# Windowed attention at the end of a convolution network: the four quarters' score products given in turn, and the weighted sums in one run

## The chip, the cores and the metric

One core of a Trainium2 chip runs the whole program, and the time is that of one execution in microseconds (us) on the device. The engines of the core have queues of their own and meet only at semaphores: PE is the matmul array, with its weight loads shown apart as PEld; DVE is the vector engine, ACT the scalar engine, POOL the general engine, and SP issues the transfers. Matmuls write PSUM, which here is used as four buffers of two banks each (`bank2`), handed out in turn; a fifth request waits until the first of the four has been read out.

## The reference, cut to what matters

Four layers run over x of shape (8, 56, 56, 192), all in fp32: two gated Toeplitz layers, a ConvNeXt block, and the windowed attention that is changed here. Each layer has a group norm ahead of it and is added to x. The attention, after a roll of the image by 3 rows and columns:

```python
q = x @ Wq; k = x @ Wk; v = x @ Wv
shp = (b, N_HEAD, nw, WS * WS, DIM_V)          # plain reshapes: (8, 6, 64, 49, 32)
q = q.reshape(shp); k = k.reshape(shp); v = v.reshape(shp)
scores = jnp.einsum('bhnqd,bhnkd->bhnqk', q, k) * DIM_V ** 0.5
scores = scores + bias                         # and masks on some windows
attn = jax.nn.softmax(scores, axis=-1)
out = jnp.einsum('bhnqk,bhnkd->bhnqd', attn, v)
out = out.reshape(b, n_h, n_w, -1) @ Wfc + bfc
```

So there are 8 x 384 small problems, each with 49 queries, 49 keys and 32 channels.

## The kernel before, in words

The attention stage (`attention`, from line 1006) is the last of the program. Its work is cut into 16 units: for each of the 8 images two halves `hh`. A unit's channels-by-token arrays `qf` and `kf` have four quarters of the image on the four groups of 32 partitions, and each quarter holds 48 problems. A unit is worked off in three thirds (`g` = 0, 1, 2), each with 16 problems of every quarter.

The four quarters of a third are split in two calls, `i` = 0 and 1. Call `i` of `scores` (line 1198) takes the quarters `i` and `i + 2`: for 8 values of `n`, two halves and two quarters `c`, a product of 32 rows (channels) by 64 columns (queries) with 49 moving columns (keys), 32 products in all, into one `bank2`. Quarter `c` has its own bank, and `half` says which 64 output partitions are written. Still inside `scores` follow the softmax's first part: DVE scales and adds the bias (line 1219) and takes the maxima (1228), POOL subtracts them (1229), ACT takes the exponentials (1230). `divide` follows: DVE sums (1237) and takes reciprocals (1238), POOL multiplies (1239). The probabilities `e` live in a ring of four buffers.

One third later they are used. `turned` transposes one `e` on PE (line 1245) and copies the result out of PSUM, the first call's on DVE (1255) and the second's on ACT (1253). `weighted` (line 1267) makes the sums: per call 32 products of 49 rows by 32 columns with 49 moving columns, into `po`; bank `par` belongs to the row half `par`. `sixths` copies `po` out on DVE (1277) and ACT (1282).

Between these, the loop places pieces of other work by hand through `give`: steps of `project`, the q, k and v products of the next unit (lines 1124, 1134 for v with its copy on ACT at 1142; 1177 for q and k, with copies on DVE at 1192 and ACT at 1190), and the two halves of `out`, the last product of the unit before (line 1293, added to x on DVE at 1304). The table `order` gives for each third how many steps stand at each of four places. In third 0 these are four v steps, in third 2 four q or k steps, in third 1 two q or k steps and both halves of `out`.

Written in order, a third on PE is: scores of call 0, piece 0, scores of call 1, piece 1, both transposes of the late third, piece 2, sums of call 0, piece 3, sums of call 1. PE takes its queue in that order. The framework's scheduler sets the order on DVE, ACT and POOL: on DVE the maxima and the sums of call 0 stand ahead of the scaling (or, in third 0, the maxima) of call 1; the copy of the transposed `e` stands ahead of the sums of call 1 in third 0 and behind them in thirds 1 and 2.

Each fp32 product of the program leaves two pairs of records, each pair a weight load and a matmul. Below, a "pair" is such a pair, so a call of `scores` has 64 pairs.

## Time and profile before

| what | value |
| --- | --- |
| median of 3 runs | 6182.19 us (6163.62 to 6187.67) |
| the profiled execution's own time | 6174.82 us |
| its span, first to last instruction | 6172.7 us |
| mean granted PE clock | 0.964 |
| attention's main loop, in the span | about 5274 to 6140 us |
| PE, PEld, DVE, ACT, POOL busy in 5274 to 6140 (866 us) | 774, 590, 520, 305, 290 us |
| scores, 6144 pairs (L1207) | PE busy 118.0 us |
| weighted sums, 6144 pairs (L1267) | PE busy 91.7 us |
| transposes (L1245) | PE busy 97.8 us |
| q and k steps (L1177) | eight groups of 40 to 59 us |
| v steps (L1124, L1134) | 95.9 and 57.2 us |
| last product (L1293) | 71.6 and 59.3 us |

Matmuls overlap in the array, so a busy figure is less than the count times the mean duration. The thirds of one unit can be told apart in the rows in order of time: third 0 has the rows of lines 1124 and 1134 between its scores, third 1 those of line 1293, third 2 four groups of line 1177.

### The profile page before, as it was taken

The page shows a single profiled execution, that of the slowest core. Times are in us where ns is not written, and L with a number is a line of the kernel's source. Part 1 is how long each engine was busy: PE and PEld are TensorE (multiplying, and loading weights), DVE is VectorE, ACT ScalarE, POOL GpSimd, SP SyncE. Part 2 cuts the span into 40 slices and gives each one's busy share as a digit, 9 for nine tenths or more (in the row PEclk, how much of TensorE's full clock was granted, in tenths as well). Part 3 has the DMA queues.
Part 4 walks back from the last instruction along what each step waited for, and adds up shares of the span by engine and source line. Part 5 has one row for each costly group of instructions (what it writes and reads, how often), then busy time and mean ns, then how long its engine had stood idle before and what let it go on. Part 6 is the DMA issues. An engine that isn't in the chain of part 4 may idle for free.

```text
span 6172.7 us, 151914 instructions
## 1 busy us (share of the span) xinstructions
PE 5666.5 (92%) x68832; PEld 4464.1 (72%) x68832; DVE 2847.8 (46%) x4858; ACT 2153.0 (35%) x2736; POOL 639.2 (10%) x833
## 2 busy tenths in 40 slices
PE   4997999899999999999889989999999999988997
PEld 3776878788778788888778878885665444666666
DVE  6663555444556444456444443242221322556555
ACT  1343444223444333344333332224323333333332
POOL 0000000000000000000000010000000100333332
PEclk9998999999999999999999999999999999999998
DMA  7799998887676788776899956663444322344442
GB/s 251 173 207 251 259 249 229 221 241 236 183 206 185 193 239 241 193 212 180 220 247 247 264 171 224 213 221 128 155 163 139 96 63 61 71 87 96 90 90 59
DMA packets 1139557, 1119.75 MB, mean 181 GB/s; under 512 B 342528, under 2 KB 1076736, under 8 KB 1123488
## 3 DMA queue, kind: packets, MB, share of 16 engines
q1 hardware_dynamic: 1103328, 909.05, 54.6%
q0 software_dynamic: 35584, 200.98, 10.4%
q8 instruction: 541, 8.86, 0.6%
q14 instruction: 104, 0.85, 0.0%
HBM read 753.79 MB, written 389.15 MB: 185 GB/s over the span
## 4 chain that ended last, share of the span: by engine, by line
PE 69%; DVE 9%; DMA 4%; ACT 3%; issue 3%; SPq 2%; POOL 1%; POOLq 0%; DVEq 0%; ACTq 0%
PE bank L256 11%; PE bank L350 7%; PE bank L903 6%; PE bank L467 6%; PE bank L477 5%; PE bank L367 5%; PE bank L764 5%; PE bank L983 4%; PE bank L482 3%; PE bank L499 3%; PE bank L997 3%; DMA qv<-t 2%; PE bank L1124 1%; PE bank L1177 1%; POOL e L1229 1%
## 5 line engine op out<-in xcount | busy, mean ns | idle before, releaser
L256 PE MATMUL bank<-wq,t 64*128 64x256 f32 (+5 forms) x8000 | 1319.6, 372 | 62.9 <-ACT t L239 42.8
L256 PEld LDWEIGHTS bank<-wq,t 64*128 64x128 f32 (+3 forms) x8000 | 1040.1, 189 | 313.4 <-issue 115.6
L275 ACT ACTIVATE t<-t 128x2048 f32<-128x2048 f32 (+1 forms) x300 | 444.2, 1488 | 777.9 <-DVE t L265 764.8
L265 DVE TENSOR_TENSOR t<-bank,wq 128x1024 f32<-128x1024 f32 (+2 forms) x500 | 540.2, 1112 | 254.1 <-PE bank L256 253.3
L357 ACT COPY ot<-bank 128x896 f32<-128x896 f32 x576 | 484.3, 920 | 384.6 <-PE bank L350 380.2
L350 PE MATMUL bank<-q,tm 56*64 56x112 f32 x18432 | 521.2, 265 | 64.2 <-issue 44.0
L511 ACT ACTIVATE t<-bank,wo 128x448 f32<-128x448 f32 x448 | 247.9, 635 | 895.3 <-PE bank L482 870.9
L350 PEld LDWEIGHTS bank<-q,tm 56*64 56x64 f32 x18432 | 479.9, 137 | 100.2 <-issue 70.3
L367 PE MATMUL bank<-ident,ot 120*128 120x120 f32 x4032 | 472.9, 276 | 76.8 <-ACT ot L357 37.2
L278 DVE TENSOR_TENSOR t<-t 128x1024 f32<-128x1024 f32 (+1 forms) x300 | 285.1, 955 | 530.8 <-ACT t L275 451.3
L367 PEld LDWEIGHTS bank<-ident,ot 120*128 120x128 f32 x4032 | 431.8, 145 | 125.9 <-ACT ot L357 42.8
L467 PE MATMUL bank<-t,wo 128*128 128x224 f32 x1792 | 393.2, 375 | 45.3 <-DVE t L449 42.3
L903 PE MATMUL bank<-z,w 128*128 128x448 f32 (+1 forms) x1344 | 413.1, 555 | 1.6 <-ACT h L912 1.6
L521 DVE SCALAR_TENSOR_TENSOR t<-bank,wo,t 128x448 f32<-128x448 f32 x112 | 76.4, 682 | 705.6 <-PE bank L506 705.6
L467 PEld LDWEIGHTS bank<-t,wo 128*128 128x128 f32 x1792 | 349.8, 202 | 63.8 <-issue 39.9
L477 PE MATMUL bank<-t,wo 128*128 128x224 f32 x1792 | 363.2, 356 | 11.3 <-issue 6.8
L538 DVE TENSOR_TENSOR t<-t,t 128x896 f32<-128x896 f32 x224 | 235.8, 1083 | 296.2 <-ACT t L511 296.1
L477 PEld LDWEIGHTS bank<-t,wo 128*128 128x128 f32 x1792 | 340.3, 192 | 19.7 <-issue 13.2
L764 PEld LDWEIGHTS bank<-xt,cm 113*112 113x112 f32 x3072 | 309.2, 178 | 36.9 <-issue 30.8
L903 PEld LDWEIGHTS bank<-z,w 128*128 128x128 f32 (+1 forms) x1344 | 182.2, 189 | 205.0 <-issue 196.8
L383 POOL DMA_DIRECT2D L_sum<-s x288 | 141.1, 496 | 1769.1 <-DVE s L373 1766.3
L764 PE MATMUL bank<-xt,cm 113*112 113x108 f32 (+2 forms) x3072 | 317.4, 263 | 4.3 <-ACT h L912 3.2
(142 smaller groups left out, 6940.1 us busy)
## 6 DMA issues: line engine op xcount, KB each, us to landing
q<-qv SPq DMA_DIRECT2D x36, 3584.0 KB
q<-qv SPq DMA_DIRECT2D x72, 1568.0 KB
L_sum<-s POOLq DMA_DIRECT2D x288, 392.0 KB, 7.6
t<-L_sum SPq DMA_DIRECT2D x112, 1008.0 KB
qv<-t SPq DMA_DIRECT2D x192, 512.0 KB
cm<-in_L_cm SPq DMA_DIRECT2D x96, 896.0 KB
tm<-L_mat SPq DMA_DIRECT2D x72, 896.0 KB
x<-t POOLq DMA_DIRECT2D x112, 336.0 KB, 5.5
```

Source lines behind the costliest of these rows:

```text
L256: nc.tensor.matmul(pp[:m, b, 256 * j : 256 * j + k], x[rows, j, 2 if part else b, s : s + m], w[rows, part, c0 + c : c0 + c + k],  start=p ...
L265: nc.vector.tensor_add(z[:m, c : c + k, :], view(pp[:m], 0, [[1, k], [256, 4]]), view(bias[:m], c0 + c, [[1, k], [0, 4]]),)
L275: nc.scalar.activation(z[:m, :n, :], z[:m, :n, :], AF.Silu)
L278: nc.vector.tensor_mul(prod[:m, :k], half[:, :, 0], half[:, :, 1])
L350: nc.tensor.matmul(pt[64 * s : 64 * s + 64, r, j * 112 : (j + 1) * 112], tm[rows, c * H : c * H + 64], q[rows, PR * s : PR * s + PR, 4 * c ...
L357: nc.scalar.copy(view(ot, 4 * g, [[112 * 32, 2], [32, 112], [1, 4]]), view(pt, 0, [[512, 2], [1, 112], [112, 4]]),)
L367: nc.tensor.transpose(pz[:, i, :120], ot[:120, at : at + 128], self.ident[:120, :120])
L467: mm(gs[c // 2][:, b, c % 2 * 256 : c % 2 * 256 + N], pw[:, 0, 128 * c : 128 * c + 128], xn[:, b], start=c % 2 == 0, stop=False,)
L477: mm(P[:, b, :N], ow[:, c, 0:128], g[:, 4 * b + c], start=c == 0, stop=False)
L511: nc.scalar.activation(pg[:, c], view(gs[i], c * 256, [[512, 2], [1, N]]), AF.Silu, bias=pb[:, 2 * i + c : 2 * i + c + 1],)
L764: nc.tensor.matmul(pc[:, 128 * e + 4 * m0 : 128 * e + 4 * m1], cm[:113, e, k, :], xt[:, m0 - 1 + k : m1 - 1 + k, c + e, :], start=n == 0 a ...
L903: nc.tensor.matmul(phs[c][:, s, :TT], w0[rows, part, at : at + 128], z[rows, Z[2 if part else s], :], start=part == flip, stop=part != flip,)
```

## The change

`scores` is called once for a third and takes two `bank2` at the start. Its innermost loop goes over the four quarters, in the order of partitions 0 to 31, 32 to 63, 64 to 95 and 96 to 127, and then over the two halves, so that eight products in a row go to eight different parts of the array (four row groups by two column halves), each row group with a bank of its own. What followed in `scores` is now `softmax`, called for both halves of the result after all 64 products. Both `divide` calls come after piece 1. `weighted` takes both transposed tiles and alternates between them, so that eight products in a row go to two row halves by four column groups; it runs once, ahead of piece 3, with `sixths` right behind it. The number of products, the pieces and their places are the same. In the changed file line 1207 is still the product of the scores, the scaling is line 1222, the transposes 1248, the weighted sums 1271, the last product 1297.

```diff
@@ -1195,22 +1195,25 @@
                     fs.append(f)
                 return v, fs[0], fs[1]
 
-            def scores(hh, g, i, qf, kf):
-
-
-                s = bank2()
+            def scores(hh, g, qf, kf):
+
+
+                ss = [bank2(), bank2()]
                 for n in range(8):
                     for half in range(2):
-                        for c in range(2):
+                        for i, c in ((0, 0), (1, 0), (0, 1), (1, 1)):
                             qd = slice(32 * (i + 2 * c), 32 * (i + 2 * c) + 32)
                             u = (16 * g + 8 * half + n) * WR
                             nc.tensor.matmul(
-                                s[64 * half : 64 * half + 64, c, n * WR : (n + 1) * WR],
+                                ss[i][64 * half : 64 * half + 64, c, n * WR : (n + 1) * WR],
                                 qf[qd, u : u + 64],
                                 kf[qd, u : u + WR],
                                 start=True,
                                 stop=True,
                             )
+                return [softmax(hh, g, i, s) for i, s in enumerate(ss)]
+
+            def softmax(hh, g, i, s):
                 var = {0: 1, 3: 2}.get((2 * i + 3 * hh + g) % 4, 0)
                 e = ering[count[0] % NE]
                 count[0] += 1
@@ -1255,22 +1258,23 @@
                     nc.vector.tensor_copy(et, ev)
                 return et
 
-            def weighted(g, i, et, v, po):
+            def weighted(g, ets, v, po):
 
                 for m in range(4):
                     for half in range(2):
                         for c in range(2):
-                            for par in range(2):
-                                at = slice(64 * par, 64 * par + WR)
-                                qr = i + 2 * c
-                                u = 4 * half + m
-                                nc.tensor.matmul(
-                                    po[32 * qr : 32 * qr + 32, par, u * WR : (u + 1) * WR],
-                                    v[at, qr, 8 * g + u, :],
-                                    et[at, 4 * c + m, 64 * half : 64 * half + WR],
-                                    start=True,
-                                    stop=True,
-                                )
+                            for i in range(2):
+                                for par in range(2):
+                                    at = slice(64 * par, 64 * par + WR)
+                                    qr = i + 2 * c
+                                    u = 4 * half + m
+                                    nc.tensor.matmul(
+                                        po[32 * qr : 32 * qr + 32, par, u * WR : (u + 1) * WR],
+                                        v[at, qr, 8 * g + u, :],
+                                        ets[i][at, 4 * c + m, 64 * half : 64 * half + WR],
+                                        start=True,
+                                        stop=True,
+                                    )
 
             def sixths(g, po, ot, oj):
 
@@ -1363,14 +1367,12 @@
                                 got = step(gen)
                         return got
 
-                    es = []
+                    es = scores(hh, g, qf, kf) if n < len(units) else []
                     for i in range(2):
-                        if n < len(units):
-                            es.append(scores(hh, g, i, qf, kf))
                         now = give(i)
                         self.norm_part()
-                        if n < len(units):
-                            divide(es[i])
+                    for e in es:
+                        divide(e)
                     if late is not None:
                         g_late, es_late, v_late = late
                         ets = [turned(e, i) for i, e in enumerate(es_late)]
@@ -1380,11 +1382,9 @@
                             ot = self.at2.tile([128, HR], F32, name="ot", bufs=1)
                             oj = self.at2.tile([128, 6, HT], F32, name="oj", bufs=1)
                         po = bank2()
-                        weighted(g_late, 0, ets[0], v_late, po)
+                        weighted(g_late, ets, v_late, po)
+                        sixths(g_late, po, ot, oj)
                     now = give(3)
-                    if late is not None:
-                        weighted(g_late, 1, ets[1], v_late, po)
-                        sixths(g_late, po, ot, oj)
                     late = (g, es, v) if es else None
                     if g == 0 and n + 3 == len(units) // 2:
                         for more in self.all_norms():
```

## The prediction

> **What bounds it now.** I read the page first, then the busy time of each engine in the attention's main loop, then PE's rows in order of time, then the chain of waits over one unit. The page says that PE is the busy engine of the whole program:

> ```profile
> PE 5666.5 (92%) x68832; PEld 4464.1 (72%) x68832; DVE 2847.8 (46%) x4858; ACT 2153.0 (35%) x2736; POOL 639.2 (10%) x833
> ```

> The change touches only the last 866 us, so that stage must be read by itself. The table of stretches (span, then busy us of PE, PEld, DVE, ACT, POOL, then granted clock, DMA share, GB/s) gives the whole loop, and two stretches that follow each other:

> ```profile
> 5274.00:6140.00 866.00, 774.08 (x21688) 590.12 (x21688) 519.82 (x837) 304.94 (x372) 290.30 (x207) 0.96 0.40 85
> ...
> 5427.90:5431.30 3.40, 1.57 (x49) 0.86 (x40) 1.34 (x2) 2.00 (x3) 1.12 (x1) 1.00 0.03 7
> 5431.30:5438.10 6.80, 6.02 (x146) 4.24 (x149) 2.56 (x5) 0.47 (x1) 1.52 (x1) 0.50 0.01 2
> ```

> PE is busy 89% of the loop; no other engine passes 60%. In the second row PE stands for over half of 3.4 us, and in the third its clock is 0.50: a pause is paid for twice. PE's rows in order of time show what a call costs (start, length of the group, pairs at the end):

> ```profile
> 5358.78 1.57 PE L1267 MATMUL bank<-et,v 49*32 49x49 f32 x128
> 5360.29 0.80 PE L1207 MATMUL bank<-f,f 32*64 32x49 f32 x40
> 5362.48 0.56 PE L1207 MATMUL bank<-f,f 32*64 32x49 f32 x24 [1.40 <-issue]
> ...
> 5470.06 2.50 PE L1293 MATMUL bank<-oj,wfc 32*64 32x224 f32 x88 [0.32 <-ACT f L1190]
> ```

> Two things are to be seen. The sums take 11 ns a pair ((1.57 - 0.2) / 127), an undisturbed call of scores (1.15 us for 64) 15 ns. And a run of such short pairs stops: after 128 + 40 pairs PE waits 1.40 us for nothing but "issue". Beside the pauses lie the packets of the instruction queue, 16 KB each, that is 128 pairs; 171 of them land in the loop. In 24 places a pause of over 1 us ends some 1.4 us after such a packet landed; these are 36 us, and with the shorter ones 47 pauses and 50 us. Instructions arrive too late. In the pause shown the last 128 pairs began at about 5359.25 (40 pairs into the sums), and PE went on at 5362.48: 3.2 us is the least time from the start of one such block to the start of the next.

> The chain of waits shows the rest, from a third 0 into a third 1:

> ```profile
> 5438.85 1.14 PE bank L1207 x64
> ...
> 5453.61 1.12 PE bank L1207 x64
> 5454.83 0.99 DVE e L1219
> 5455.84 0.98 DVE mx L1228
> ...
> 5456.98 1.53 POOL e L1229
> 5458.53 0.88 ACT e L1230
> 5459.43 0.98 DVE sm L1237
> ...
> 5460.61 0.93 DVE e L1219
> 5461.56 0.98 DVE mx L1228
> ...
> 5462.69 1.55 POOL e L1229
> 5464.27 0.88 ACT e L1230
> 5465.18 0.98 DVE sm L1237
> ```

> Third 0 (up to 5453.6) is all PE. Then the chain leaves PE and runs through the softmax of call 0 and, after it, that of call 1, because DVE's queue has the scaling of call 1 (5460.61) behind the sums of call 0. In third 1 this holds up the additions of line 1304 and so the second half of the last product; in third 2 it holds up the copy of the transposed tile, and so the sums.

> **The change, part by part, for one unit.** Times below count from the start of a third's scores.

> Scores. The starts of a call's 64 pairs spread over 0.93 us in the trace; on 4 parts of the array these are 16 rounds of 58 ns, and 0.2 us follow to the next group. With 128 pairs on 8 parts the rounds stay 16: 1.15 us in place of 2.30. That eight products can run is shown by line 1293: 88 pairs of 224 columns, the same 32 by 64 shape over four row groups and two halves, in 2.50 us are (2.50 - 0.35) / 87 = 25 ns a pair, while one pair streams some 190 ns. The bounds are 1.15 us (full gain) and 2.1 us (15 ns a pair as now); I take the first, on the nearest shape.

> Sums. 64 pairs take 0.83 us with the step to the next group; xb's steps of line 1177, in the same 64 by 32 shape over two row halves and four column groups, issue their pairs about 6.7 ns apart. 128 pairs at 6.7 ns and 0.2 us are 1.05 us in place of 1.66. Bounds: 0.9 and 1.55.

> [...]

> Softmax. DVE now has both scalings, both maxima, then (in the thirds with q or k steps) a copy of line 1192, then the sums. With durations and gaps of the chain above: scalings start at 1.3 and 2.3, maxima at 3.3 and 4.3, POOL subtracts 4.45 to 5.97 and to 7.5, ACT's exponentials end at 6.9 and 8.4, the sums at 7.9 and 9.4, the reciprocals at 9.9. The first call's values come later than now, the second's earlier, and POOL and ACT work under DVE. The values are used a third later, so the end of `divide` is covered by some 10 us of work on PE. Two PSUM buffers are now taken at once. In third 0 the one for the sums is that of the second v step, whose copy (0.80 us) on ACT moves behind the second exponential, to 9.2; the sums need it at 11.0 at the earliest. The store of that copy on SP's queue follows as late; it is read a unit later.

> Third 0. Now 5438.85 to 5453.54, 14.7 us. After: PE needs scores 1.15, three pieces and transposes 3 x 2.36 + 1.76, so it is at the sums at 10.0; but the transposed copy (1.09 us) now stands behind the second call's sums on DVE and ends at 11.0. PE waits 1.0, and the piece and the next scores queue behind that wait. Then sums 1.05 and a piece 2.36: 14.45. Nearly nothing gained; the wait replaces the time saved.

> Third 2. Now, without a stop: scaling 1.29, call 0's round 5.78 (5454.83 to 5460.61), call 1's 5.54 (to 5466.15), copy 1.0, so the sums start at 13.6; then 0.83 + 2.36 + 0.83 = 17.6. After: as third 0, 14.45.

> Third 1. Now 5453.54 to 5473.99, 20.45. After: sums and the reciprocal end at 9.7, the additions (2.55) at 12.3, the copies of lines 1192 and 1190 at 13.35, the second half of the last product 2.5, the weighted sums 1.05: 16.9.

> A unit falls from 52.75 to 45.8 us, by 6.95; for 15 full units (the first has no late sums) 104 us. No transfer is added. POOL's and SP's queues keep their work; POOL's two multiplications move behind both subtractions.

> Stops for instructions. The same pairs now come in denser runs: 128 of sums, a piece, 128 of scores. Take third 2 into third 0, with 64 pairs left of the block begun and one block landed: the block ends 0.45 us into the sums and the one after next may start at 3.7; sums and q step use the landed block by 3.4 (0.3 lost), the scores use the next at once (to 4.9), and the following piece waits until 6.95: 2.0 us. Between thirds 1 and 2, where no piece stands, it is 2.1 + 0.25; into third 1, with only 16 pairs in the piece, 0.7. That is 5.4 us a unit for this phase; the phase moves, and blocks that take 3.6 rather than 3.25 us raise it to 7.5. I take 6.9, of which PE's waits for DVE hide some. Against 50 us now that is 110, so 60 us are given back. Below: nothing given back, if the stops all fall into the waits. Above: every third stops for a whole block, 48 x 3.25 = 156, 106 more.

> The clock. Of the 3.4 us stretches in the loop some 19 are at 0.50 now. More pauses of 2 us make more of them, while third 2's wait of 2.4 us, which brought the one shown, goes. I take 12 more at 1.3 us: 16 us. Bounds: 10 fewer (-13) and 30 more at 1.7 (51).

> Sum: 6174.8 - 104 + 60 + 16 = 6147, against the profiled execution's own 6174.8, which is 7.4 below the median of the three runs.

> [...]

> **The rivals.**
> 1. The stops hide in the waits: only a small part is given back. For it: in thirds 0 and 2 PE has 1.0 us of slack before the sums. Against it: the runs are longer than two blocks. 104 less 0 to 40: 6071 to 6110.
> 2. Slower: instructions set the pace. Unit by unit 1408 pairs are 11 blocks; if every third stops for a block (+106) and 30 more stretches run at half clock (+51), it is 6228. It decides from the point where stops and clock together add more than 7 us a unit. For it: the pauses above, and the half clock that follows them. Against it: 11 blocks need only 36 of 45.8 us.
> 3. The change does not do what it says: eight products run no faster than four. Then a unit loses 5.2 of its 6.95 us and keeps the softmax's part, 26 us, of which denser runs still cost some 15: 6164. Against it: line 1293.

> **How the numbers follow.** The forecast, 6115 to 6175 with its own bounds on stops and clock, 0.48; rival 1, 0.17; rival 2 and anything between it and the forecast, 0.25; rival 3, 0.10. A measurement of this kernel tells about 0.5%, 31 us, from no change. Against the median, faster means below 6151: rival 1 and a little more than half of the forecast, 0.44. Slower means above 6213: half of rival 2, 0.13. The rest, 0.43, is within. The range from 6080 to 6210 leaves out the lower third of rival 1 and the upper half of rival 2.

> **What the profile after would show.** Line 1207 in groups of 128 pairs that take 1.15 us where undisturbed, line 1271 in 1.05; if 2 and 1.5, rival 3. DVE's two scalings back to back, and sums of line 1271 starting 11 us after the scores. Pauses by "issue" ahead of and inside lines 1207, 1271 and 1177 grown to about 110 us, and more stretches at 0.50; if these stay near 50 us, rival 1. It would all be wrong if a block of instructions came much faster or slower in denser runs than the 3.2 us seen here, or if four row groups writing four banks slowed each other.

## The result and the profile after

The change makes no difference that this measurement can tell: 6186.29 us, the median of 20 runs (6168.06 to 6203.30), against 6184.22 for the kernel before on the same chip. The ratio is 1.0005, with a 95% interval from 0.9995 to 1.0015. A faster kernel was forecast, 6147, and the gain of 35 us against the median of the three runs before did not come.

The first lines of the page of the kernel after, its span and the busy time of the engines:

```profile
span 6184.8 us, 151962 instructions
PE 5636.1 (91%) x68832; PEld 4429.0 (72%) x68832; DVE 2848.5 (46%) x4858; ACT 2151.7 (35%) x2736; POOL 637.5 (10%) x833
```

The instructions are the same in number, and PE is busy 30 us less. The span is 12.1 us longer than that of the profiled execution before. In this execution the loop began 7 us later (5281.4 in place of 5274.5), before any line that the change touches; from the first third's scores to the last third's it took 868.7 us in place of 857.9. The table of stretches for the whole loop (span, busy us of PE, PEld, DVE, ACT and POOL, granted clock, DMA share, GB/s):

```profile
5274.00:6150.00 876.00, 741.94 (x21720) 550.91 (x21712) 514.73 (x836) 303.28 (x373) 286.74 (x206) 0.93 0.42 84
```

PE was busy 774 of 866 us and is now busy 742 of 876: the array works less and waits more, and the clock granted in the loop went from 0.96 to 0.93. What it waits for stands in the table of waits over the same stretch (engine and line, what it waited for, us in total, times, longest). First before:

```profile
PEld bank L1177 <- issue: 52.8, 138, 2.6
PEld bank L1207 <- issue: 40.1, 69, 1.7
PE bank L1207 <- issue: 21.5, 23, 1.6
PE bank L1245 <- DVE ra L1304: 19.7, 13, 2.1
PEld bank L1267 <- ACT et L1253: 18.5, 12, 3.0
```

and after:

```profile
PEld bank L1177 <- issue: 95.3, 198, 3.3
PEld bank L1207 <- issue: 59.3, 51, 3.4
PE bank L1207 <- issue: 49.7, 33, 3.3
PE bank L1177 <- issue: 31.5, 21, 2.9
PE bank L1207 <- DVE f L1192: 15.1, 16, 1.1
PEld bank L1271 <- ACT et L1256: 11.4, 11, 1.2
```

PEld and PE wait side by side, so the two are not added up. The waits on the softmax (line 1245 on line 1304, line 1267 on 1253) shrink or go, and the waits on "issue", in which the profile shows nothing that PE waits for, take their place. Short ones, 0.15 to 0.3 us each, stand inside the q and k steps; all of PE's longer ones, over 0.35 us (38 before, 69 after), end where a block of instructions begins, as the last section says. Line 1207 has a longer wait besides, 16 times 1 us for DVE's copy of line 1192 (3.1 us in all before). PE's rows in order of time show both (start, length, line, pairs at the end, the idle time in brackets):

```profile
5444.87 1.37 PE L1271 MATMUL bank<-et,v 49*32 49x49 f32 x128 [0.73 <-DVE et L1258]
5446.17 1.55 PE L1124 MATMUL bank<-Wv,xa 128*112 128x192 f32 x8
...
5466.20 1.38 PE L1271 MATMUL bank<-et,v 49*32 49x49 f32 x128
5467.51 0.46 PE L1207 MATMUL bank<-f,f 32*64 32x49 f32 x26
5469.75 1.50 PE L1207 MATMUL bank<-f,f 32*64 32x49 f32 x102 [1.79 <-issue]
5471.19 2.54 PE L1177 MATMUL bank<-xa,Wq 128*32 128x224 f32 x25
...
5487.56 1.54 PE L1207 MATMUL bank<-f,f 32*64 32x49 f32 x128 [1.05 <-DVE f L1192]
5489.03 1.55 PE L1124 MATMUL bank<-Wv,xa 128*112 128x192 f32 x8
```

The 128 pairs of an undisturbed third's scores lead to the next group after 1.47 us (5487.56 to 5489.03), the sums after 1.30 (5444.87 to 5446.17); before it was twice 1.08 and twice 0.83. So eight products do run together, and faster. But after 128 + 26 of them PE stands for 1.79 us, and the 25 pairs of line 1177 that follow take 2.54 us, at a granted clock of 0.50 (5471.2 to 5473.7), where 32 take 1.54 at full clock (5475.45). The chain of waits over a third 0, after:

```profile
5432.17 1.29 DVE xa L1099 x2
5433.46 0.54 DVE f L1192
...
5434.05 1.58 PE bank L1207 x91
...
5436.57 0.97 DVE e L1222
5437.54 0.88 DVE mx L1231
...
5440.05 1.53 POOL e L1232
...
5441.61 0.88 ACT e L1233
...
5442.52 0.97 DVE sm L1240
...
5443.77 0.96 DVE et L1258
...
5444.87 1.37 PE bank L1271 x82
```

One softmax round in place of two, and the sums 10.8 us after the scores: as the prediction has it. The two lines at the top are what it does not have. DVE's queue holds the normalizing of line 1099 ahead of the last k step's copy, the next unit's scores wait for that copy, and the piece that stood between now stands ahead of it.

For all kernels below, three numbers were counted in the records of the profiled execution: the mean length of a unit (14 units, from scores to scores), the time lost in pauses that end where a block of 128 pairs of instructions (16 KB) begins (those of more than 0.35 us), and the time in the loop at the half clock. The pauses depend on how they are measured: counted from the start of one matmul to the start of the next, all come out within 8 us of the table, and the idle time of PE alone is smaller, 41 us before and 102 after.

| kernel | median us | ratio to before, 95% interval | unit us | pauses on blocks us | half clock us |
| --- | --- | --- | --- | --- | --- |
| before | 6184.22 | | 55.59 | 48.4 | 64.9 |
| after | 6186.29 | 1.0005 (0.9995 to 1.0015) | 56.48 | 125.1 | 126.3 |
| e1_scores_only | 6193.53 | 1.0024 (1.0010 to 1.0038) | 57.78 | 126.9 | 160.4 |
| e2_sums_only | 6238.78 | 1.0093 (1.0066 to 1.0119) | 59.88 | 70.2 | 139.9 |
| e4_four_at_a_time | 6192.14 | 1.0013 (1.0000 to 1.0026) | 57.16 | 95.3 | 167.3 |
| e5_piece_first | 6220.96 | 1.0064 (1.0045 to 1.0083) | 59.69 | 156.1 | 232.1 |
| x1_before_half | 6201.24 | 1.0018 (1.0004 to 1.0032) | 57.93 | 7.4 | 204.8 |
| x2_after_half | 6039.48 | 0.9760 (0.9736 to 0.9783) | 46.87 | 27.8 | 17.1 |
| e6_after_mixed | 6204.05 | 1.0024 (1.0010 to 1.0038) | 57.55 | 139.8 | 150.2 |
| e7_before_mixed | 6219.32 | 1.0051 (1.0030 to 1.0072) | 59.38 | 87.2 | 143.4 |
| x6_half_padded | 6186.82 | 1.0015 (0.9999 to 1.0030) | 57.92 | 110.0 | 129.7 |
| x7_half_four | 6019.64 | 0.9744 (0.9716 to 0.9772) | 45.76 | 10.0 | 6.8 |
| e11_piece_first_third2 | 6191.39 | 1.0019 (1.0004 to 1.0035) | 57.85 | 139.6 | 180.9 |
| e8_after_block | 6158.43 | 0.9962 (0.9945 to 0.9978) | 54.09 | 50.9 | 68.3 |
| e13_block_again | 6158.72 | 0.9964 (0.9952 to 0.9976) | 54.50 | 50.9 | 71.7 |
| e12_block_four | 6113.65 | 0.9895 (0.9876 to 0.9915) | 52.06 | 37.2 | 54.6 |
| e14_block_before | 6279.58 | 1.0156 (1.0135 to 1.0177) | 62.82 | 12.8 | 109.2 |
| e15_block_piece | 6092.48 | 0.9855 (0.9835 to 0.9876) | 50.09 | 43.2 | 23.9 |

Each ratio is to runs of the kernel before on the same chip (medians of these from 6179 to 6188 us).

### The profile page after: what moved, and what is told of

Read it like the earlier page. It is cut to its first block, busy times and chain, and to the rows that moved or that the text cites. A ratio compares the mean times of both kernels' runs of the same rounds, so it can differ in the third digit from the quotient of the medians.

```text
span 6184.8 us, 151962 instructions
## 1 busy us (share of the span) xinstructions
PE 5636.1 (91%) x68832; PEld 4429.0 (72%) x68832; DVE 2848.5 (46%) x4858; ACT 2151.7 (35%) x2736; POOL 637.5 (10%) x833
## 3 DMA queue, kind: packets, MB, share of 16 engines
q1 hardware_dynamic: 1103328, 909.05, 54.6%
q0 software_dynamic: 35584, 200.98, 10.4%
## 4 chain that ended last, share of the span: by engine, by line
PE 72%; DVE 6%; DMA 4%; issue 4%; ACT 3%; SPq 1%; POOL 1%; DVEq 0%; ACTq 0%; POOLq 0%
PE bank L256 11%; PE bank L350 6%; PE bank L903 6%; PE bank L467 6%; PE bank L477 5%; PE bank L367 5%; PE bank L764 5%; PE bank L983 4%; PE bank L1177 4%; PE bank L482 3%; PE bank L499 3%; PE bank L997 2%; DMA qv<-t 2%; PE bank L1297 2%; PE bank L1207 1%
## 5 line engine op out<-in xcount | busy, mean ns | idle before, releaser
L477 PEld LDWEIGHTS bank<-t,wo 128*128 128x128 f32 x1792 | 340.2, 192 | 21.4 <-issue 13.6
```

Of the source, the lines that this page charges most:

```text
L477: mm(P[:, b, :N], ow[:, c, 0:128], g[:, 4 * b + c], start=c == 0, stop=False)
```

## The experiments

Two theories stood at the start. A: the joined order is worth what was forecast, but PE is not given instructions fast enough, so that whatever is saved comes back as pauses and half clock. B: it is the placement, above all the sums in one run and the wait for line 1192.

### Each half of the change alone

`e1_scores_only` keeps the joined scores and undoes the sums:

```diff
-                        weighted(g_late, ets, v_late, po)
-                        sixths(g_late, po, ot, oj)
+                        weighted(g_late, 0, ets[0], v_late, po)
                     now = give(3)
+                    if late is not None:
+                        weighted(g_late, 1, ets[1], v_late, po)
+                        sixths(g_late, po, ot, oj)
```

> The scores of all four quarters in one go, eight products at a time, with both divisions late; the weighted sums in two calls on either side of piece 3, as before. Theory A (supply): denser runs wait for blocks of instructions, and pauses then halve the clock. The run of 64 sums and 128 scores without a piece still outruns the blocks: pauses on instructions of 90 to 120 us in the loop (before 50, after 125), time within 10 us of before. Theory B (placement): the loss of the whole change is the sums in one run ahead of piece 3, which lays open the copy of the last q or k step ahead of the next scores (about 20 us of waits in the profile after). That copy is covered again here: 20 to 35 us faster than before.

`e2_sums_only` is the kernel before with the sums of the kernel after, the mirror image of that diff.

> The weighted sums in one run of 128 pairs, eight at a time, ahead of piece 3; the scores in two calls as before. Theory A (supply): 128 sums, a piece, 64 scores, little denser than before: pauses 55 to 80 us. The sums save 0.3 us in each of 48 thirds, 14 us; the uncovered copy costs 1.3 us in 15 units, 20 us: 5 to 20 us slower than before. Theory B (placement): the whole loss is here: 15 to 35 us slower than before.

Measured: 1.0024 and 1.0093. The scores alone, on which B set a gain, are 11 us slower than before by the medians, with the same pauses as the kernel after (126.9 us): B falls as the whole story, and A's figures (10 us, 120 us) are just missed. The sums alone cost 57 us, more than either theory had. PE's rows of that kernel, in a third 0, show why:

```profile
5447.34 0.28 PE L1268 MATMUL bank<-et,v 49*32 49x49 f32 x4
5449.41 1.35 PE L1268 MATMUL bank<-et,v 49*32 49x49 f32 x124 [1.80 <-ACT et L1253]
5450.69 2.50 PE L1124 MATMUL bank<-Wv,xa 128*112 128x192 f32 x8
```

The run of sums needs both transposed tiles at once; with the softmax in two rounds the second tile's copy on ACT is late, PE stands for 1.80 us, and the v step after it takes 2.50 us in place of 1.55; 139.9 us of this kernel's loop run at half clock, 64.9 before. The two halves of the change are not separable: one run of sums without the joined softmax makes a wait.

### Fewer products on the array at a time; the open copy covered

`e4_four_at_a_time` keeps every place of the change but gives the products in groups of four:

```diff
-                for n in range(8):
+                for i, n in [(i, n) for i in range(2) for n in range(8)]:
                     for half in range(2):
-                        for i, c in ((0, 0), (1, 0), (0, 1), (1, 1)):
+                        for c in range(2):
...
-                for m in range(4):
+                for i, m in [(i, m) for i in range(2) for m in range(4)]:
```

> The changed kernel with the products of the scores and of the sums given quarter pair by quarter pair, four at a time, everything else as changed. Theory A (supply): PE would wait for the blocks anyway, so slower products only fill the pauses: pauses fall to about 80 us and the time is within 12 us of the changed kernel. Theory B (placement): the eight at a time are worth their 0.54 us and 0.23 us in 48 thirds, 37 us: 30 to 45 us slower than the changed kernel.

`e5_piece_first` gives the last piece of every third ahead of the sums, so that the sums stand over the copy of line 1192; `e11_piece_first_third2`, whose diff follows, does it in third 2 alone:

```diff
+                    if g == 2:
+                        now = give(3)
                     if late is not None:
                         po = bank2()
                         weighted(g_late, ets, v_late, po)
                         sixths(g_late, po, ot, oj)
-                    now = give(3)
+                    if g < 2:
+                        now = give(3)
```

> The changed kernel with piece 3 ahead of the sums instead of behind them, so that 128 sums and 128 scores stand in a row and the copy of the last q or k step lies beside the sums. Theory A (supply): the wait for the copy goes (20 us less), but 256 pairs in a row outrun the blocks in every third: pauses of 130 to 160 us in the loop, time within 15 us of the changed kernel. Theory B (placement): 20 us faster than the changed kernel, with the same pauses.

> The changed kernel with piece 3 ahead of the sums in third 2 only, so that the copy of the last q or k step lies beside 1.3 us of sums. The wait of the next scores for that copy goes, 15 times 1.05 to 1.3 us, 16 to 20 us. Theory A (supply): 128 sums and 128 scores stand in a row once more in each unit, pauses grow by 10 to 25 us: within 15 us of the changed kernel. Theory B (placement): 16 to 20 us faster than the changed kernel.

Measured: 1.0013, 1.0064 and 1.0019. Slower groups on the array change next to nothing: pauses are 30 us shorter (that slower groups leave the blocks more time to arrive is a guess, which no run shows by itself), and 41 us more run at half clock. Covering the copy takes a wait of 15 us away and gains nothing: in e5 in every third, in e11 at the end of each unit, the sums and the next scores now follow each other without a piece between, 256 short pairs in a row, and the pauses rise to 156 and 140 us. In e11 this is what theory A expected; e5 is some 36 us slower than the change, more than either theory allowed, and 106 us more of it runs at half clock. In this kernel a wait that is removed is not won; PE then runs into the next block that has not landed.

### Half the products, on both kernels

To take the supply of instructions away as a limit, both kernels were run with half the products of scores and sums, each with about twice the moving columns: `x1_before_half` and `x2_after_half` (the diff of the second). They leave out half of the products, so what they compute is not the attention.

```diff
-                for n in range(8):
+                for n in range(0, 8, 2):
...
-                                ss[i][64 * half : 64 * half + 64, c, n * WR : (n + 1) * WR],
+                                ss[i][64 * half : 64 * half + 64, c, n * WR : (n + 2) * WR],
...
-                    for half in range(2):
+                    for half in range(1):
```

> The kernel before with half as many products in the scores and in the sums, each moving twice the columns (98 for 49, 113 for 49): each second window's scores take the first one's queries and the two halves share one block of v, so the attention's numbers are not the reference's. 768 of a unit's 1408 pairs become 384, 8 blocks of instructions instead of 11. Theory A (supply): the pauses of 48 us nearly go (below 10), the half clock shrinks with them; the array's time falls by some 17 us besides: 45 to 75 us faster than before. Theory B (placement): only the array's 17 us: 10 to 25 us faster.

> The changed kernel with the same halving of products. Theory A (supply): with the instructions no longer short (pauses below 30 us) the change shows its worth: 16 rounds of four products less per third and the joined softmax, less the open copy; 60 to 100 us faster than the kernel before with the same halving. Theory B (placement): the change is still worth nothing: within 25 us of the kernel before with the same halving.

Then `x6_half_padded` puts the number of instructions of x2 back, with products of a single moving column that nothing reads, and `x7_half_four` gives x2's products in groups of four.

```diff
+                    for half in range(2):
+                        for i, c in ((0, 0), (1, 0), (0, 1), (1, 1)):
...
+                                ss[i][64 * half : 64 * half + 64, c, 400 + n : 401 + n],
+                                qf[qd, u : u + 64],
+                                kf[qd, u : u + 1],
```

> The changed kernel with half as many products of twice the columns (as in the run that was 149 us faster), and for each product a second one of a single column into an unused place of the bank, so that PE's instructions are as many as in the changed kernel while the array gets hardly more work; the attention's numbers are again not the reference's. Theory A (supply): the blocks are short again; pauses on instructions above 90 us, half clock above 90 us, 90 to 150 us slower than the kernel with half the products. Theory C (array time): that kernel was faster because its array time is smaller; below 35 us slower than it, pauses below 50 us.

> The changed kernel with half the products, given four at a time instead of eight, all else the same. With instructions no longer short, both theories expect the packing's own worth: rounds of 84 and 97 ns, eight more for the scores and eight more for the sums in each of 48 thirds, 1.4 us a third, some of it behind the softmax's chain: 25 to 65 us slower than eight at a time. If the packing is worth nothing even then, below 10 us.

Measured: on the kernel before the halving is worth nothing (1.0018), on the kernel after 2.4% (0.976), and with the number of instructions put back it is gone (1.0015). That is theory A: x6 adds to x2 only products of one column, and some 150 us lie between them (147 by the medians, 158 by the ratios). The added pairs are not free on PE itself: an undisturbed group of scores takes 1.67 us to the next group in place of 0.99, one of sums 1.63 in place of 1.00, up to 63 us in 48 thirds. The rest is pauses, 82 us more, and half clock, 113 us more, of which up to half is loss. Between x1 and x2, which differ by the change alone, lie 162 us, more than the 60 to 100 expected and the 104 of the prediction. That is what the joined order is worth where instructions arrive in time, but in a kernel with less work on PE: PE's waits for the softmax in thirds 1 and 2 (lines 1245 and 1267 on DVE) are 89 us in x1 and 34 in the kernel before, so for the full kernel the figure is too high.

x1 was expected to gain and did not: a miss. Its pauses on blocks are down to 7.4 us, but it runs 205 us at half clock. PE's rows of x1, out of a third 1 and a third 2:

```profile
5425.65 1.13 PE L1245 MATMUL bank<-ident,e 113*113 113x113 f32 x8 [2.77 <-DVE ra L1304]
5426.96 5.69 PE L1293 MATMUL bank<-oj,wfc 32*64 32x224 f32 x96 [0.19 <-DVE ra L1304]
...
5448.12 1.73 PE L1267 MATMUL bank<-et,v 49*32 49x113 f32 x32 [3.28 <-DVE et L1255]
5449.78 2.84 PE L1177 MATMUL bank<-xa,Wk 128*32 128x224 f32 x32
```

With less work on PE the softmax's two rounds end last in thirds 1 and 2: PE stands for 2.77 and 3.28 us, and what follows runs at half clock (96 pairs of line 1293 in 5.69 us, 32 of line 1177 in 2.84, against 2.53 and 1.54 at full). The joined round takes these waits away, and the half clock with them: 205 us become 17.

x7 was expected to be slower than x2 by its array time, and was not (0.9744 and 0.9760, with intervals that overlap): another miss, and the first sign that eight at a time is worth nothing here even where instructions are ample.

### Other steps between the groups

`e6_after_mixed` and `e7_before_mixed` spread v steps and q and k steps over the thirds, so that the dense thirds get steps with few instructions:

```diff
+                steps = vs_ + qk
+                if mixed:
+                    steps = [vs_[0], qk[0], vs_[1], qk[1], qk[2], vs_[2], qk[3], qk[4], qk[5], vs_[3]]
```

> The changed kernel with the ten steps of the projection in another order: v, q, v, q in third 0, q and v in third 1, three of k and the last v in third 2. Pairs per third go from 336, 544, 528 to some 432, 496, 480, and no q or k step stands ahead of the next unit's scores, so no copy lies open. Theory A (supply): pauses fall from 125 to about 90 us and the half clock with them, 20 us of open copies go: 25 to 55 us faster than the changed kernel. Theory B (placement): the 20 us of the copies alone.

> The kernel before with the steps of the projection in the same new order (v, q, v, q; q, v; three of k and the last v). Theory A (supply): pauses fall from 48 us to about 30 and the half clock a little: 5 to 30 us faster than before. Theory B (placement): within 12 us of before, since no copy lay open.

Measured: 1.0024 and 1.0051, misses both. The instructions are as many as before, and pauses still rise, to 139.8 and 87.2 us: spreading the steps did not thin them out. Third 0 grows longer in the mean (from 15.3 to 16.3 us in e6, from 14.7 to 16.6 in e7), and in both kernels mostly by another wait: its sums now wait for ACT, for the copy of the transposed tile in e6 (15.0 us in the loop) and for the copy of a q or k step in e7 (21.7 us).

### Fewer instructions with nothing left out

A unit has 1408 pairs. `e8_after_block` makes the weighted sums with half as many: the transposed probabilities of two windows are copied into a tile whose other entries are zero, so that one product of 113 rows and 98 columns gives both windows. Copies on ACT, one more for each tile, pay for it; the unit has 1216 pairs. Beside what the diff shows, the tile of the bias is smaller and the softmax's maxima and sums have four buffers in place of six.

```diff
-                    nc.vector.tensor_copy(et, ev)
+                    nc.vector.tensor_copy(et[0:64, :, :, 0], ev[0:64, :, :, :WR])
+                nc.scalar.copy(et[64:113, :, :, 1], ev[64:113, :, :, :WR])
...
+                                nc.tensor.matmul(
+                                    po[32 * qr : 32 * qr + 32, half, m * 2 * WR : (m + 1) * 2 * WR],
+                                    v[0:113, qr, 8 * g + 4 * half + m, :],
+                                    ets[i][:, 4 * c + m, half],
```

> The changed kernel with the weighted sums of two problems in one product: the transposed tile is copied into a block form (upper rows into one half of the columns, lower rows into the other, zeros elsewhere), so that 113 rows by 32 columns with 98 moving columns do what two products of 49 rows did. 1216 pairs a unit instead of 1408, computed in full. It takes two more copies on ACT in a third (0.9 us each). Theory A (supply): pauses fall from 125 to 60 to 90 us, the half clock with them, 25 to 70 us faster than the changed kernel and than before. Theory B (placement): no faster than the changed kernel; the longer copies hold up the sums, 0 to 30 us slower.

Measured: 0.9962, some 24 us faster than the kernel before and 27 faster than the kernel after by the ratios, at the low end of what was expected: pauses and half clock fall back to about what they were before the change. `e12_block_four` is the same with the scores in groups of four (the first part of e4's diff), and `e13_block_again` is e8 once more on the same chip.

> The kernel with block-form sums (e8), but the scores' products given in groups of four: both calls still one after the other at the start of the third, with the quarters i and i + 2 first and then the others. If eight products at a time are worth nothing where instructions are the limit, the time is within 8 us of e8, since what the scores lose (16 to 48 x 0.7 us = up to 34 us of array time) comes out of the pauses on instruction blocks, which should fall from 51 us by about as much. If they are worth their array time, it is 20 to 34 us slower than e8.

> The kernel with block-form sums once more, beside its twin with groups of four, for a comparison on one chip. From its first run: 0.9945 to 0.9978 of before, whichever theory holds.

Measured: 0.9895 against 0.9964. Groups of four are 45 us faster than groups of eight, which neither theory expected. DVE's rows over a third 0, in the kernel with eight (e13):

```profile
5438.81 1.86 DVE L1230 SCALAR_TENSOR_TENSOR e<-bank,bias 128x784 f32<-128x784 f32 x2 [1.69 <-PE bank L1215]
5440.59 1.83 DVE L1239 TENSOR_REDUCE mx<-e 128x16 f32<-128x784 f32 x2
```

and with four (e12):

```profile
5476.42 0.98 DVE L1230 SCALAR_TENSOR_TENSOR e<-bank,bias 128x784 f32<-128x784 f32 x1 [1.34 <-PE bank L1215]
5477.43 0.97 DVE L1239 TENSOR_REDUCE mx<-e 128x16 f32<-128x784 f32 x1
5478.32 0.97 DVE L1230 SCALAR_TENSOR_TENSOR e<-bank,bias 128x784 f32<-128x784 f32 x1
5479.32 0.97 DVE L1239 TENSOR_REDUCE mx<-e 128x16 f32<-128x784 f32 x1
```

With eight at a time both calls' scores end together, and DVE takes both scalings and then both maxima; the first maxima are there 4.4 us after the scores began (5437.18 to 5440.59 and 0.97). With four the first call's scores end early, its scaling starts 0.35 us sooner, and its maxima follow at once: they are there after 3.26 us (5475.14 to 5478.40), and POOL, ACT and all behind them start from that. Of these 1.12 us, 0.35 are the earlier scaling and the other 0.77 are DVE's order, which the framework's scheduler set: in every third the kernels with eight have both scalings ahead of both maxima, and those with four take them in turn. No run gives eight products at a time with the other order, so the two were not told apart. What PE waits for ahead of its sums, first with eight, then with four:

```profile
PE bank L1277 <- ACT etb L1267: 40.5, 45, 6.0
PE bank L1277 <- ACT etb L1267: 12.6, 24, 3.7
```

In PE's rows the sums of a third 0 begin 11.50 us after the scores with eight and 10.82 with four (median and least agree in both), and the median third 0 takes 16.03 and 15.34 us. The loop is shorter by 38 us (843.2 to 805.1). Of these 11 are the 0.69 us in 16 thirds 0, 13.7 are shorter pauses on blocks, and up to 8.5 come from 17 us less at half clock; the last few were not told apart. So the array's time for the scores was not what bounded this kernel: with four they take 1.90 us to the next group in place of 1.47, and the kernel is faster. Giving the array more products at a time went together with a later softmax of the first call.

`e14_block_before` is the block form in the arrangement of the kernel before, and `e15_block_piece` is e12 with e11's edit.

> The block-form sums in the arrangement of the kernel before: scores in two calls around piece 0, sums in two calls around piece 3, softmax in two rounds; the same 1216 pairs a unit as e12. If, once instructions are fewer, what the change is worth is the joined softmax round and the joined placement, this kernel is 20 to 70 us slower than e12, near 6140 to 6180. If e12 owes its time to the block form alone, both are within 10 us.

> e12 (block form, groups of four) with the last q or k step of third 2 given ahead of the sums, so that they cover its copy of line 1192 and PE does not wait 1.04 us for it ahead of the next unit's scores. If that wait is time now that instructions are fewer, 10 to 20 us faster than e12, some 0.987 of before. If the pauses and half clock take it back, as they did in the kernel after, the same within 8 us.

Measured: 1.0156 and 0.9855. Between e14 and e12, with the same 1216 pairs a unit and the scores in the same groups of four (the sums go to two parts of the array in turn in e14, to four in e12), the joined arrangement is worth 2.6%, some 160 us; 20 to 70 were expected. The waits of e14 over its loop:

```profile
PEld bank L1276 <- ACT etb L1267: 99.7, 41, 3.9
PE bank L1276 <- ACT etb L1267: 85.3, 31, 3.7
PE bank L1256 <- DVE ra L1313: 25.6, 14, 2.2
```

Its pauses on blocks are only 12.8 us; PE stands for the softmax and the copies behind it. Since the block form loads ACT more than the kernel before did, this is an upper figure for the arrangement there; x1 and x2 gave the same size in another way.

In e15 the wait for the copy of line 1192 (line 1200 in this file) is gone, and here it is time: a third 2 falls from 18.72 to 16.77 us in the mean, half clock from 54.6 to 23.9 us, and the kernel is some 20 to 25 us faster than e12 (21 by the medians, 25 by the ratios, which are from two comparisons). The end of a unit in PE's rows of e15:

```profile
5467.91 1.55 PE L1185 MATMUL bank<-xa,Wk 128*32 128x224 f32 x32
5469.38 0.96 PE L1185 MATMUL bank<-xb,Wk 64*32 64x224 f32 x32
5470.27 1.56 PE L1277 MATMUL bank<-etb,v 113*32 113x98 f32 x64
5471.77 2.08 PE L1215 MATMUL bank<-f,f 32*64 32x49 f32 x128
5473.78 1.55 PE L1132 MATMUL bank<-Wv,xa 128*112 128x192 f32 x8
```

Sums and scores follow the k step with no pause. The same edit was worth nothing in e11, where pauses and half clock grew instead (by 14.5 and 54.6 us against the kernel after). Of the kernels that leave nothing out this is the fastest, 1.45% under the kernel before.

## Why the prediction was wrong

The time lay in the range, which reached to both sides of no change, and a result within the noise had been given 0.43, hardly less than the 0.44 for faster; the forecast of a gain did not hold. The step that failed in its mechanism is third 2, taken over from third 0; the price of the half clock, and perhaps that of the stops, was too small. Step by step:

**Scores, 1.15 us in place of 2.30, and sums, 1.05 in place of 1.66: right in kind, off in size.** By the same measure (start to the next group) scores went from 2.16 to 1.47 and sums from 1.66 to 1.30. The array takes eight at once, but not at the assumed pace: in the records of single pairs the rounds of eight come some 60 to 80 ns apart at the start of a call, for some 30 pairs, and then pairs start mostly 8 or 17 ns apart, so that 128 take 1.32 us where 0.93 was assumed. Whether the array or the giving of pairs sets that pace was not told apart. The 6.7 ns assumed for the sums is the step inside bursts of four or eight pairs; a whole step of xb gives 32 pairs in 0.89 us, 28 ns a pair. A unit's array time falls by 3.15 us, not 5.28. As e4 shows, this had no price in the result, and in the block form (e12) groups of four were even faster.

**The softmax and third 0: right.** The sums start 10.82 us after the scores at the least and 11.04 in the median of thirds 0 (11.0 forecast); a third 0 takes 14.44 at the least (14.45 forecast) and 15.18 in the median. **Third 1, 16.9:** 16.41 in the median of x2, where few pauses stand and the products are half as many, and 20.11 after. **"After: as third 0, 14.45", for third 2, is a step that failed.** It takes 16.38 even in x2 and 20.70 after, 6.2 us over the forecast: in a mean third 2 PE stands 3.3 us in pauses on blocks and 0.94 in a wait for DVE's copy, and 4.6 us run at half clock. The working carried third 0's list over and left out what ends third 2: the copy of line 1192, behind line 1099 on DVE, ahead of the next unit's scores. Before, half the sums stood over it (3.1 us of waiting in the whole loop); now nothing does (15.1 us). The prediction names the queues that DVE's steps are moved past, but not the one whose cover was moved away.

**"I take 6.9", the stops for instructions, 60 us given back: right in kind, the largest in size, and right or low in size.** Pauses on blocks went from 48.4 to 125.1 us, 77 more; by the idle time of PE alone it is 61 more. **"I take 12 more at 1.3 us: 16 us", the clock: low, by up to a factor of two.** 61 us more were spent at half clock, 18 stretches of 3.4 us; work took about twice as long there (in x1 96 pairs of line 1293 in 5.69 us, 2.53 at full, and 32 of line 1177 in 2.84, 1.54 at full), so up to half of the 61, 31 us, is loss, an estimate from these rows.

The terms so corrected are -104 + 12 + 77 + 31 = +16 us, or 0 with 61 for the stops; the 12 are the wait for the copy, 15.1 - 3.1. Measured was +10.8 in the loop. Within the size of these estimates nothing is left over. The -104 itself no run measures in the full kernel; that the joined order is worth that much rests on x1 and x2 and on e14 and e12, whose 160 us are upper figures. Three costs, one or two listed too low and one not listed, ate it up. Of the rivals, the second had the mechanism right, "instructions set the pace", and its condition too, as near as can be told: it decides from 7 us a unit, and stops and clock came to (77 + 31) / 15 = 7.2, or 6.1 with the smaller count. That put the kernel at the turning point, not at 6228. The first, stops hidden in the waits, falls: they came on top. The third, eight no faster than four, falls on the array and holds in the time.

## What to carry to other kernels

Count instructions as work with a rate of its own: in the loops of before and after no two packets of 128 pairs started less than 3.28 us apart, 26 ns a pair, while an undisturbed run of scores used them up in 10.4. In these dense runs time saved on a wait went to the next block of instructions that had not landed: the same edit is worth nothing in e11, where pauses grew by 14.5 us, and 20 us in e15, where the instructions are fewer. When an edit joins two calls, ask what the first call's result was doing while the second was computed; in the block form, where the products in groups of eight came with a later first result, groups of four were 45 us faster; in the kernel after (e4) the grouping made no difference. When a piece is moved, write down for each copy that stood beside it what covers it now.
